# Attention scores with keys on partitions, an unshifted exponential and a general path behind a branch

## Chip, cores and metric

One NeuronCore of one Trainium2 chip. The metric is the device time of one execution in microseconds (us); where several were timed, the median is quoted with the number of executions.

## The reference, cut to what matters

Eight images of 512 channels and 32 x 32 = 1024 positions, all in fp32. First multi-head attention over positions (8 heads of 64 channels), then a second, linear non-local layer and a batch normalization over everything.

```python
q = _conv1x1(x, Wq, bq).reshape(B, h, d, H * W)          # B=8, h=8, d=64, H*W=1024
k = _conv1x1(x, Wk, bk).reshape(B, h, d, H * W)
v = _conv1x1(x, Wv, bv).reshape(B, h, d, H * W)
attn = jax.nn.softmax(jnp.einsum('bhdn,bhdm->bhnm', q, k) * scale, axis=-1)
out = jnp.einsum('bhnm,bhdm->bhdn', attn, v).reshape(B, C, H, W)
x = x + _conv1x1(out, Wp, bp)
# layer 1
theta_x, phi_x, g_x = ...                                 # 1x1 products of x to 256 channels
f_div_C = jnp.einsum('bcn,bdn->bcd', theta_x, phi_x) / n
y = jnp.einsum('bcd,bdn->bcn', f_div_C, g_x)
z = _conv1x1(y, W_w, W_b) + x
return batch_norm(z) * gamma + beta                       # over images and positions
```

## The kernel before

Scores have queries on partitions. Two heads make a pair: they sit in partitions 0 to 63 and 64 to 127, so their score products use the two row halves of TensorE's array. The maximum of a row is taken on VectorE, the exponential with its sum on ScalarE, the scaling on GpSimd. As the value product needs keys on partitions, every attention row is then transposed on TensorE and copied out of PSUM. PSUM holds two score buffers of two banks, and in single banks two for transposes and two for all other products.

```python
psS = ...(name="psS", bufs=2, PSUM)    # score buffers [128, 1024], 2 banks each
psT = ...(name="psT", bufs=2, PSUM)    # transposes
psM = ...(name="psM", bufs=2, PSUM)    # all other products

def scores(p, i, q, k):                # pair p, block i of 128 queries
    ps = [psS.tile([P, N], F32, tag="s") for j in range(2)]
    for nh in range(NH):
        for j in range(2):
            r = slice(j * D, (j + 1) * D)
            nc.tensor.matmul(ps[j][:, nh*512:(nh+1)*512], q[r, i*P:(i+1)*P], k[r, nh*512:(nh+1)*512], ...)
    for j in range(2):
        nc.vector.tensor_reduce(nm, ps[j], AX.X, ALU.max, negate=True)
        nc.scalar.activation(e, ps[j], AF.Exp, bias=nm, accum_out=sm)
        nc.vector.reciprocal(rs, sm)
        nc.gpsimd.tensor_scalar(e, e, rs, 1.0, ALU.mult, ALU.mult)

def values(p, i, es):
    for j in range(2):
        for half in range(2):
            for m in range(NB // 2):
                nc.tensor.transpose(pt[:, m, :], es[j][:, mb * P:(mb + 1) * P], ident)
            # half 0 is copied out by VectorE, half 1 by ScalarE
    if g == GRP - 1:                   # after every second block
        for m in range(NB):
            for j in range(2):         # the two heads: column halves of the array
                nc.tensor.matmul(ps[j*D:(j+1)*D, :GRP*P], v[:, m, h*D:(h+1)*D], pts[j][:, m, :], ...)
# ... cut: projections, layer 1, batch normalization; 5 of 8 images are spilled to DRAM and reloaded
```

Of the kernel before, what the change touches and what calls it, by code (L numbers as in the profile page):

```python
# [8 lines left out]
F32 = mybir.dt.float32  # L9
AF = mybir.ActivationFunctionType  # L10
ALU = mybir.AluOpType
AX = mybir.AxisListType

P = 128
HEADS = 8
EPS = 1e-5


@with_exitstack
def attention_nonlocal_kernel(ctx: ExitStack, tc: tile.TileContext, a: dict, out: bass.AP):  # L20
# [3 lines left out]
    CC = C // P  # channel chunks  # L24
    NB = N // P  # position blocks
    NH = N // 512  # position halves, one PSUM bank each
# [4 lines left out]
    KEEP = 3  # batches whose values stay in SBUF  # L31
    GRP = 2  # position blocks that one attention-value product takes
# [3 lines left out]
    big = ctx.enter_context(tc.tile_pool(name="big", bufs=2))  # L36
    w1 = ctx.enter_context(tc.tile_pool(name="w1", bufs=1))
    w2 = ctx.enter_context(tc.tile_pool(name="w2", bufs=2))
    w3 = ctx.enter_context(tc.tile_pool(name="w3", bufs=3))
    small = ctx.enter_context(tc.tile_pool(name="small", bufs=4))  # L40
    psS = ctx.enter_context(tc.tile_pool(name="psS", bufs=2, space=bass.MemoryType.PSUM))
    psT = ctx.enter_context(tc.tile_pool(name="psT", bufs=2, space=bass.MemoryType.PSUM))
    psM = ctx.enter_context(tc.tile_pool(name="psM", bufs=2, space=bass.MemoryType.PSUM))
    dram = ctx.enter_context(tc.tile_pool(name="dram", bufs=1, space=bass.MemoryType.DRAM))

    x_v = a["x"].rearrange("b (cc p) h w -> b p cc (h w)", p=P)
    out_v = out.rearrange("b (cc p) h w -> b p cc (h w)", p=P)

# [6 lines left out]
    def load_w(name):  # L55
        k, m = a[name].shape
        t = const.tile([P, k // P, m], F32, tag=name, name=name)
        nc.scalar.dma_start(t, a[name].rearrange("(c p) f -> p c f", p=P))
        return t

    def load_col(name):
        t = const.tile(list(a[name].shape), F32, tag=name, name=name)
        nc.sync.dma_start(t, a[name])
        return t

# [1 line left out]
    wv = load_w("WvT")  # L67
    x_next = load_x(0)
    wq, wk = load_w("WqT"), load_w("WkT")
    bv_b = const.tile([P, C], F32, tag="bv_b", name="bv_b")  # L70
    nc.sync.dma_start(bv_b, a["bv"].partition_broadcast(P))
    bq, bk, bp, gb, wb = (load_col(n) for n in ("bq", "bk", "bp", "gb", "Wb"))
    gamma, beta = load_col("gamma"), load_col("beta")
    wp = load_w("WpT")
    tpb = const.tile([P, 2 * CI], F32, tag="tpb", name="tpb")
    nc.sync.dma_start(tpb[:, :CI], a["theta_b"].partition_broadcast(P))
    nc.sync.dma_start(tpb[:, CI:], a["phi_b"].partition_broadcast(P))
# [3 lines left out]
    wg, ww = load_w("WgT"), load_w("WwT")  # L81

    ident = const.tile([P, P], F32, tag="ident", name="ident")
    make_identity(nc, ident)
    eps = const.tile([P, 1], F32, tag="eps", name="eps")
    nc.vector.memset(eps, EPS)
    stats = const.tile([P, CC, B * NH, 6], F32, tag="stats", name="stats")
    spill = [dram.tile([P, CC, N], F32, tag=f"spill{b}", name=f"spill{b}") for b in range(B - KEEP)]

    def mm(m, n, pairs, name):  # L90
        """The sum of products of (lhsT, rhs) over pairs, in one PSUM bank."""
        ps = psM.tile([P, 512], F32, tag="mm", name=name)
        for i, (l, r) in enumerate(pairs):
            nc.tensor.matmul(ps[:m, :n], l, r, start=(i == 0), stop=(i == len(pairs) - 1))  # L94
        return ps[:m, :n]

# [1 line left out]
    def layer0(b, xt):  # L98
        v = big.tile([P, NB, C], F32, tag="big", name=f"v_{b}")  # [position, channel]
        for i in range(NB):  # L100
            ps = mm(P, C, [(xt[:, c, i * P:(i + 1) * P], wv[:, c, :]) for c in range(CC)], f"pv_{b}_{i}")
            nc.vector.tensor_tensor(v[:, i, :], ps, bv_b, ALU.add)

        o = big.tile([P, CC, N], F32, tag="big", name=f"o_{b}")

        def make_qk(p):
            q = w2.tile([P, N], F32, tag="q", name=f"q_{b}_{p}")
            k = w2.tile([P, N], F32, tag="k", name=f"k_{b}_{p}")
            for nh in range(NH):
                s = slice(nh * 512, (nh + 1) * 512)  # L110
                co = slice(p * P, (p + 1) * P)
                ps = mm(P, 512, [(wq[:, c, co], xt[:, c, s]) for c in range(CC)], f"pq_{b}_{p}_{nh}")
                nc.vector.tensor_scalar(q[:, s], ps, bq[:, p:p + 1], float(D) ** -0.5, ALU.add, ALU.mult)  # L113
                ps = mm(P, 512, [(wk[:, c, co], xt[:, c, s]) for c in range(CC)], f"pk_{b}_{p}_{nh}")
                nc.scalar.activation(k[:, s], ps, AF.Identity, bias=bk[:, p:p + 1])  # L115
            return q, k

        def scores(p, i, q, k):
            """The normalized attention rows of position block i, for the two heads of pair p."""
            ps = [psS.tile([P, N], F32, tag="s", name=f"ps_{b}_{p}_{i}_{j}") for j in range(2)]  # L120
            for nh in range(NH):
                for j in range(2):
                    r = slice(j * D, (j + 1) * D)
                    nc.tensor.matmul(  # L124
                        ps[j][:, nh * 512:(nh + 1) * 512],
                        q[r, i * P:(i + 1) * P],
                        k[r, nh * 512:(nh + 1) * 512],
                        start=True, stop=True,
                    )
            res = []  # L130
            for j in range(2):
                nm = small.tile([P, 1], F32, tag="nm", name=f"nm_{b}_{p}_{i}_{j}")
                nc.vector.tensor_reduce(nm, ps[j], AX.X, ALU.max, negate=True)  # L133
                e = w3.tile([P, N], F32, tag="e", name=f"e_{b}_{p}_{i}_{j}")
                sm = small.tile([P, 1], F32, tag="sm", name=f"sm_{b}_{p}_{i}_{j}")
                nc.scalar.activation(e, ps[j], AF.Exp, bias=nm, accum_out=sm)  # L136
                rs = small.tile([P, 1], F32, tag="rs", name=f"rs_{b}_{p}_{i}_{j}")
                nc.vector.reciprocal(rs, sm)  # L138
                nc.gpsimd.tensor_scalar(e, e, rs, 1.0, ALU.mult, ALU.mult)  # L139
                res.append(e)  # L140
            return res

        pts = {}

        def values(p, i, es):
            """Transposes the attention rows; after each GRP blocks, multiplies them with v."""
            g = i % GRP
            if g == 0:
                for j in range(2):
                    pts[j] = w3.tile([P, NB, GRP * P], F32, tag="pt", name=f"pt_{b}_{p}_{i}_{j}")  # L150
            for j in range(2):
                for half in range(2):
                    pt = psT.tile([P, NB // 2, P], F32, tag="t", name=f"pst_{b}_{p}_{i}_{j}_{half}")
                    for m in range(NB // 2):
                        mb = half * (NB // 2) + m
                        nc.tensor.transpose(pt[:, m, :], es[j][:, mb * P:(mb + 1) * P], ident)  # L156
                    dst = pts[j][:, half * (NB // 2):(half + 1) * (NB // 2), g * P:(g + 1) * P]
                    if half == 0:
                        nc.vector.tensor_copy(dst, pt)  # L159
                    else:  # L160
                        nc.scalar.copy(dst, pt)  # L161
            if g == GRP - 1:
                ps = psM.tile([P, 512], F32, tag="mm", name=f"pav_{b}_{p}_{i}")
                for m in range(NB):
                    for j in range(2):
                        h = 2 * p + j
                        nc.tensor.matmul(  # L167
                            ps[j * D:(j + 1) * D, :GRP * P],
                            v[:, m, h * D:(h + 1) * D],
                            pts[j][:, m, :],  # L170
                            start=(m == 0), stop=(m == NB - 1),
                        )
                i0 = i - (GRP - 1)
                nc.vector.tensor_copy(o[:, p, i0 * P:(i + 1) * P], ps[:, :GRP * P])  # L174

        qk = make_qk(0)
        qk_next = None
        pending = None
        for p in range(NPAIR):
            for i in range(NB):  # L180
                es = scores(p, i, *qk)
                if pending is not None:
                    values(*pending)
                pending = (p, i, es)
                if i == NB // 2 and p + 1 < NPAIR:
                    qk_next = make_qk(p + 1)
# [137 lines left out]
```

## Time and profile before

| | before |
|---|---|
| time, 4 executions | 3519.7 to 3556.3 us, median 3554.9 |
| profiled execution | span 3518.2 us, mean granted clock 0.987 |
| TensorE busy | 3226.5 us, 92% |
| after the last matmul | 65 us, DMA share 0.93 to 1.02 at 374 to 411 GB/s |

Three groups of its attention matter for the change (columns: line, engine, operation, operands, count; busy us, mean ns of one; idle time before and what ended it). In timelines further down the first two columns are the start and the duration in us, and brackets give the idle time before and what ended it; PE is TensorE, PEld its weight loads, DVE VectorE, ACT ScalarE, POOL GpSimd:

```profile
L156 PE MATMUL pst<-ident,e 128*128 128x128 f32 x4096 | 560.1, 280 | 17.5 <-ACT pt L161 10.5
L133 DVE TENSOR_REDUCE nm<-ps 128x1 f32<-128x1024 f32 x512 | 602.8, 1219 | 294.0 <-PE ps L124 294.0
L124 PE MATMUL ps<-k,q 64*128 64x512 f32 x2048 | 793.9, 637 | 199.6 <-ACT e L136 199.6
```

4096 transposes, a VectorE pass over all scores, and 200 us in which TensorE stood before a score product until an exponential had freed its buffer.

### The profile page before, as it was taken

The page shows a single profiled execution, that of the slowest core. Times are in us where ns is not written, and L with a number is a line of the kernel's source. Part 1 is how long each engine was busy: PE and PEld are TensorE (multiplying, and loading weights), DVE is VectorE, ACT ScalarE, POOL GpSimd, SP SyncE. Part 2 cuts the span into 40 slices and gives each one's busy share as a digit, 9 for nine tenths or more (in the row PEclk, how much of TensorE's full clock was granted, in tenths as well). Part 3 has the DMA queues.
Part 4 walks back from the last instruction along what each step waited for, and adds up shares of the span by engine and source line. Part 5 has one row for each costly group of instructions (what it writes and reads, how often), then busy time and mean ns, then how long its engine had stood idle before and what let it go on. Part 6 is the DMA issues. An engine that isn't in the chain of part 4 may idle for free.

```text
span 3518.2 us, 33619 instructions
## 1 busy us (share of the span) xinstructions
PE 3226.5 (92%) x13632; PEld 1653.5 (47%) x13632; DVE 1329.1 (38%) x2087; ACT 984.7 (28%) x1699; POOL 574.5 (16%) x518
## 2 busy tenths in 40 slices
PE   8998999999999999999999999999999999999992
PEld 3445444444444544444444444444444445444451
DVE  2344234442344423443234432444324442244424
ACT  2334013330233202332033320333103331133304
POOL 1222012220122201221022210222102220022200
PEclk9999999999999999999999999999999999999996
DMA  4000000000000010000100001000000000000016
GB/s 150 1 1 1 13 35 1 1 1 34 15 1 1 1 48 0 1 1 1 48 0 1 1 1 48 1 1 1 1 0 1 1 1 0 0 1 1 1 48 262
DMA packets 20538, 63.51 MB, mean 18 GB/s; under 512 B 2848, under 2 KB 4640, under 8 KB 20384
## 3 DMA queue, kind: packets, MB, share of 16 engines
q1 hardware_dynamic: 11808, 38.29, 2.9%
q10 hardware_dynamic: 8576, 23.07, 1.7%
q8 instruction: 108, 1.77, 0.2%
q14 instruction: 46, 0.38, 0.0%
HBM read 34.09 MB, written 27.26 MB: 17 GB/s over the span
## 4 chain that ended last, share of the span: by engine, by line
PE 78%; DVE 10%; ACT 9%; issue 1%; DMA 1%; ACTq 0%; SPq 0%
PE ps L124 16%; PE pav L167 15%; DVE nm L133 9%; ACT e L136 9%; PE pst L156 8%; PE pq L94 6%; PE pv L94 6%; PE pp L94 6%; PE pk L94 6%; PE ptp L94 6%; PE pg L94 3%; PE pz L94 3%; PE pf L94 2%; PE pwf L94 1%; DMA z<-spill 1%
## 5 line engine op out<-in xcount | busy, mean ns | idle before, releaser
L139 POOL TENSOR_SCALAR e<-e,rs 128x1024 f32<-128x1024 f32 x512 | 573.8, 1121 | 2779.4 <-DVE rs L138 2779.3
L124 PE MATMUL ps<-k,q 64*128 64x512 f32 x2048 | 793.9, 637 | 199.6 <-ACT e L136 199.6
L136 ACT ACTIVATE e<-ps,nm 128x1024 f32<-128x1024 f32 x512 | 573.7, 1121 | 857.9 <-DVE nm L133 857.9
L133 DVE TENSOR_REDUCE nm<-ps 128x1 f32<-128x1024 f32 x512 | 602.8, 1219 | 294.0 <-PE ps L124 294.0
L156 PEld LDWEIGHTS pst<-ident,e 128*128 128x128 f32 x4096 | 439.6, 141 | 394.6 <-issue 291.8
L156 PE MATMUL pst<-ident,e 128*128 128x128 f32 x4096 | 560.1, 280 | 17.5 <-ACT pt L161 10.5
L167 PE MATMUL pav<-pt,v 128*64 128x256 f32 x4096 | 522.7, 382 | 0.0
L159 DVE COPY pt<-pst 128x512 f32<-128x512 f32 x512 | 351.1, 686 | 329.9 <-PE pst L156 329.9
L124 PEld LDWEIGHTS ps<-k,q 64*128 64x128 f32 x2048 | 252.5, 188 | 473.1 <-ACT e L136 263.4
L167 PEld LDWEIGHTS pav<-pt,v 128*64 128x64 f32 x4096 | 319.8, 137 | 166.2 <-DVE pt L159 28.8
L161 ACT COPY pt<-pst 128x512 f32<-128x512 f32 x512 | 297.7, 581 | 178.8 <-PE pst L156 178.8
L115 ACT ACTIVATE k<-pk,bk 128x512 f32<-128x512 f32 x64 | 44.0, 687 | 800.4 <-PE pk L94 800.4
L174 DVE COPY o<-pav 128x256 f32<-128x256 f32 x128 | 54.3, 424 | 472.8 <-PE pav L167 472.8
L94 PE MATMUL pq<-x,WqT 128*128 128x512 f32 x512 | 232.7, 597 | 0.0
L94 PE MATMUL pv<-WvT,x 128*128 128x512 f32 x512 | 222.7, 596 | 9.1 <-DMA WvT<-in_WvT_dram 9.1
L94 PE MATMUL pk<-x,WkT 128*128 128x512 f32 x512 | 230.2, 592 | 0.0
L94 PE MATMUL pp<-o,WpT 128*128 128x512 f32 x512 | 221.9, 594 | 0.0
L94 PE MATMUL ptp<-wtp,x 128*128 128x512 f32 x512 | 221.0, 592 | 0.0
L94 PEld LDWEIGHTS pv<-WvT,x 128*128 128x128 f32 x512 | 97.8, 191 | 132.0 <-issue 122.8
L113 DVE TENSOR_SCALAR q<-pq,bq 128x512 f32<-128x512 f32 x64 | 48.0, 750 | 294.7 <-PE pq L94 294.7
L94 PEld LDWEIGHTS pk<-x,WkT 128*128 128x128 f32 x512 | 97.3, 190 | 122.5 <-issue 122.5
L94 PEld LDWEIGHTS ptp<-wtp,x 128*128 128x128 f32 x512 | 97.3, 190 | 122.5 <-issue 122.5
(37 smaller groups left out, 1170.9 us busy)
## 6 DMA issues: line engine op xcount, KB each, us to landing
x<-in_x_dram SPq DMA_DIRECT2D x32, 512.0 KB, 5.8
spill<-x SPq DMA_DIRECT2D x20, 512.0 KB, 2.6
z<-spill SPq DMA_DIRECT2D x20, 512.0 KB, 6.8
out_dram<-z ACTq DMA_DIRECT2D x20, 512.0 KB, 5.4
out_dram<-x ACTq DMA_DIRECT2D x12, 512.0 KB, 5.2
WvT<-in_WvT_dram ACTq DMA_DIRECT2D x1, 1024.0 KB, 8.4
WqT<-in_WqT_dram ACTq DMA_DIRECT2D x1, 1024.0 KB, 13.9
WkT<-in_WkT_dram ACTq DMA_DIRECT2D x1, 1024.0 KB, 16.0
```

The costliest lines, as they stand in the source:

```text
L94: nc.tensor.matmul(ps[:m, :n], l, r, start=(i == 0), stop=(i == len(pairs) - 1))
L113: nc.vector.tensor_scalar(q[:, s], ps, bq[:, p:p + 1], float(D) ** -0.5, ALU.add, ALU.mult)
L115: nc.scalar.activation(k[:, s], ps, AF.Identity, bias=bk[:, p:p + 1])
L124: nc.tensor.matmul(ps[j][:, nh * 512:(nh + 1) * 512], q[r, i * P:(i + 1) * P], k[r, nh * 512:(nh + 1) * 512], start=True, stop=True,)
L133: nc.vector.tensor_reduce(nm, ps[j], AX.X, ALU.max, negate=True)
L136: nc.scalar.activation(e, ps[j], AF.Exp, bias=nm, accum_out=sm)
L139: nc.gpsimd.tensor_scalar(e, e, rs, 1.0, ALU.mult, ALU.mult)
L156: nc.tensor.transpose(pt[:, m, :], es[j][:, mb * P:(mb + 1) * P], ident)
L159: nc.vector.tensor_copy(dst, pt)
L161: nc.scalar.copy(dst, pt)
L167: nc.tensor.matmul(ps[j * D:(j + 1) * D, :GRP * P], v[:, m, h * D:(h + 1) * D], pts[j][:, m, :], start=(m == 0), stop=(m == NB - 1),)
L174: nc.vector.tensor_copy(o[:, p, i0 * P:(i + 1) * P], ps[:, :GRP * P])
```

## The change

Scores are made transposed: keys on partitions, queries along the free dimension. The exponential then has the layout that the value product wants as its moving operand, and transposes and copies fall away. A row's maximum would now lie across partitions, so the shift is left out. To make that safe, each pair's scores are bounded by the sum over channels of max|q| max|k|; if any bound exceeds 60, the queries are zeroed and a complete second program (`shifted`) runs at the end behind a branch. Sums come from additions on VectorE and a product with ones, and the division is applied to the output. PSUM now holds three score buffers of two banks, used for all large products too, and two single banks. TensorE's order is pinned; other products stand where a result is awaited. The core of the diff:

```diff
-    psS = ctx.enter_context(tc.tile_pool(name="psS", bufs=2, ...PSUM))
-    psT = ...bufs=2;  psM = ...bufs=2
+    psS = ctx.enter_context(tc.tile_pool(name="psS", bufs=3, space=PSUM))
+    psO = ctx.enter_context(tc.tile_pool(name="psO", bufs=2, space=PSUM))
+    RUN = 4      # steps (pair, query half, key block) in a run
+    LEAD = 128
+    def pe(ins): tc.keep_in_program_order(ins)
+    # queries_keys(): max|k|, max|q| by tensor_reduce, their product is `peak`
+    def bound_scores(b, p, q, k, peak):
+        pe(nc.tensor.matmul(ps[:, 0, :1], heads, peak, start=True, stop=True))
+        nc.vector.tensor_scalar(gate, ps[:, 0, :1], BOUND, 1.0, ALU.is_le, ALU.mult)
+        nc.gpsimd.tensor_scalar(q, q, gate, 1.0, ALU.mult, ALU.mult)
+    def scores(run):
+        for p, h, m in run:
+            for j in range(2):
+                pe(nc.tensor.matmul(ps[:, j, :], k[r, m*P:(m+1)*P], q[r, h*512:(h+1)*512], ...))
+            nc.scalar.activation(e, ps, AF.Exp)
+            nc.vector.tensor_tensor(acc, acc, e, ALU.add)
+    def columns(ps, lhsT, rhs, start, stop, lead):
+        for j in range(2):
+            if lead and j == 0:        # first product of a run in two pieces, 128 and 384 columns
+                pe(nc.tensor.matmul(to[:, :LEAD], l, r[:, :LEAD], ...))
+                pe(nc.tensor.matmul(to[:, LEAD:], l, r[:, LEAD:], ...))
+            else:
+                pe(nc.tensor.matmul(to, l, r, ...))
+    def normalize(p, h, lead):
+        columns(ps, lambda j: ones, lambda j: acc[:, j, :], True, True, lead)
+        nc.vector.reciprocal(ri, ps)
+        nc.vector.tensor_tensor(o[:, p, s], o[:, p, s], ri, ALU.mult)
+    for i, run in enumerate(runs):
+        scores(run)
+        if i % 4 == 3 ...: bound_scores(b, p + 1, *qk[p + 1])
+        if i: weighted(runs[i - 1], due)   # value products; starts with normalize() when one is due
+        if i % 4 == 2 ...: qk[p + 1] = queries_keys(b, xt, p + 1)
+    # next image's values and queries fill gaps of layer 1; 6 images are spilled and reloaded early
+    sound = nc.values_load(count, min_val=0, max_val=P)
+    with tc.If(sound < P): shifted(tc, a, out)
```

## The prediction

VectorE's 12.9 us per half pair and the gate's 7.9 us count the additions, whose time came from no trace, and so do the 26 to 30 us per pair and the 46% of the span. Read from the trace of the kernel before: 512 `pq` instructions for 256 fp32 products, hence two for each; the reciprocal's 177 - 153 = 24 ns for three more elements. The 0.4 us for a bound, the 0.1 us of scattered waits per run and the 2 to 4 us for landing and the branch are estimates, and so are the 3 us of slow clock; for these, that trace has the first weight loads 0.85 us apart instead of 0.43 until 11.9 us, and a granted clock of 0.50 from 57 to 60.

> **What bounds the kernel now.** I read the page first, for who is busy.
>
> ```profile
> span 3518.2 us, 33619 instructions
> PE 3226.5 (92%) x13632; PEld 1653.5 (47%) x13632; DVE 1329.1 (38%) x2087; ACT 984.7 (28%) x1699; POOL 574.5 (16%) x518
> PE 78%; DVE 10%; ACT 9%; issue 1%; DMA 1%; ACTq 0%; SPq 0%
> ```
>
> TensorE is at 92%, and the chain that ended last is its work for 78%. The other 19% are VectorE and ScalarE steps (the maximum, the exponential) that TensorE waits for. So two things count: how much TensorE has to do, and whether something still interrupts it. The groups of instructions give the first, with a warning: matmul spans overlap, so I do not take durations from means but from distances between starts. For these I read TensorE's timeline inside the attention of image 1.
>
> ```profile
> 601.46 3.60 PE L94 MATMUL pk<-x,WkT 128*128 128x512 f32 x8
> 604.89 3.60 PE L94 MATMUL pq<-x,WqT 128*128 128x512 f32 x8
> ...
> 613.76 1.09 PE L156 MATMUL pst<-ident,e 128*128 128x128 f32 x8
> 615.60 1.12 PE L124 MATMUL ps<-k,q 64*128 64x512 f32 x2 [0.75 <-ACT e L136]
> 616.65 1.09 PE L156 MATMUL pst<-ident,e 128*128 128x128 f32 x8
> 617.68 1.98 PE L124 MATMUL ps<-k,q 64*128 64x512 f32 x6
> 619.59 1.09 PE L156 MATMUL pst<-ident,e 128*128 128x128 f32 x8
> 621.43 1.12 PE L124 MATMUL ps<-k,q 64*128 64x512 f32 x2 [0.75 <-ACT e L136]
> 622.48 1.09 PE L156 MATMUL pst<-ident,e 128*128 128x128 f32 x8
> 623.50 4.08 PE L167 MATMUL pav<-pt,v 128*64 128x256 f32 x32
> 627.52 1.98 PE L124 MATMUL ps<-k,q 64*128 64x512 f32 x6
> 629.43 1.09 PE L156 MATMUL pst<-ident,e 128*128 128x128 f32 x8
> ```
>
> Four readings. (1) Eight full-array instructions take 604.89 - 601.46 = 3.43 us, 0.4288 each; an fp32 product is two of them, 0.857 us for 512 columns. (2) The value product is 32 instructions of 256 columns. At the full-array rate they would take 32 x 0.214 = 6.86 us; they take 627.52 - 623.50 = 4.02, so the two heads, in two column halves of the array, do run side by side. (3) Of a block's eight score instructions only four overlap: six take 1.91 us and two, alone, 1.05, while four perfect pairs would be 4 x 0.4288 = 1.72. The scheduler had to break the second pair because its PSUM buffer was still read by the exponential (the 0.75 us). (4) The pattern repeats every two blocks: 629.43 - 613.76 = 15.67 us. There are 128 such repeats (8 images x 4 pairs x 4), so attention proper is 128 x 15.67 = 2006 us. Full-array products are 3136 instructions of 512 columns (x0.4288 = 1345 us) and 256 of 256 columns (55 us): 1400 us. Together 3406; the rest is start (9 us to the first matmul), edges of each image and the end.
>
> The end I read from windows of busy time (columns: stretch, length, PE, PEld, DVE, ACT, POOL busy, granted clock, DMA share, GB/s):
>
> ```profile
> 3460.00:3480.00 20.00, 0.00 (x0) 0.00 (x0) 13.52 (x19) 12.49 (x13) 0.00 (x0) 0.50 1.00 374
> 3480.00:3500.00 20.00, 0.00 (x0) 0.00 (x0) 6.50 (x8) 9.12 (x9) 0.00 (x0) 0.50 1.02 411
> 3500.00:3518.00 18.00, 0.00 (x0) 0.00 (x0) 0.00 (x0) 10.41 (x10) 0.00 (x0) 0.50 0.93 379
> ```
>
> After the last matmul (3453) 65 us follow, and the DMA engines are full at about 390 GB/s: 16.8 MB go out while 12 chunks of spilled z (6.3 MB) still come in.
>
> [...] heads in column halves start late, 4.02 us against 3.43 for perfect pairs. [...] Eight transposes of 128 columns need 8 x 0.107 = 0.86 us at the rate of reading 1, and from 622.48 to 623.50 1.02 passed: I estimate 0.1 to 0.16 us per change. [...] The trace has it for one element (153 ns) and for four (177 ns): 8 ns an element[...]. So a reciprocal of 512 columns should cost about 4.2 us. [...]
>
> **The change, part by part.** *The branch to the general path is not taken.* I computed the bound from the reference's inputs: 18.6 to 20.5 over all images and head pairs, against a limit of 60. The second program costs only its reading of a count and one branch per engine.
>
> *Removed from TensorE:* all transposes, 4096 x 0.107 = 440 us plus their mode changes, and the exponential's 0.75 us, twice in 15.67 (192 us). Also removed: VectorE's maximum (602.8 us) and its copies (351), ScalarE's copies (298) and accumulator reads (103), GpSimd's scaling (574).
>
> *Scores.* Per image there are 64 steps (pair, half, key block), each one pair of 512-column products in the two row halves. Runs of four steps: 8 x 0.4288 = 3.43, plus about 0.19 for the change of mode in and out, 3.62 us. 128 runs: 463 us. Each step has its own two-bank buffer of three, so nothing breaks the pairs: the fourth step starts 2.57 us into a run and needs the first exponential to be over (product done at about 1.05, plus 1.12: 2.2).
>
> *Value product.* Runs of four steps in column halves: 8 x 0.4288, plus the late start of the second head (0.42 us in the trace's first such group; the 128-column lead may shorten it) and a change: about 3.95 us. 128 runs: 506 us.
>
> *Sums.* Sixty-four pairs of products with ones: 64 x 0.86 = 55 us. New, on TensorE.
>
> *Unchanged:* 1400 us of full-array products, now emitted in an order that puts other products wherever a result is awaited (next image's values and queries).
>
> *Bounds.* 32 tiny products with what they wait for, 0.4 us each: 13 us.
>
> *Other engines.* A score and a value run together last 7.6 us. ScalarE has four exponentials then, 4.5 us. VectorE has, per half pair (15.2 + 0.86 us, plus 13.7/2 of queries and keys in three of four pairs), [...] one reciprocal of 4.3 and a multiplication of 0.6, 12.9 us, and for the next pair q's eviction and two maxima, 3.7 us per pair. So 26 to 30 us of 32 to 46. VectorE is the nearest rival, but its work has runs of slack. The gate is the tightest: from the end of q's product, eviction 1.3, maximum 1.2, [...] gate, GpSimd 1.12, 7.9 us; the scores that need q come at about 8.5.
>
> *End.* Six images reload during the last image's second layer (12.6 MB, some 32 us at 390 GB/s, of about 90 us); 16.8 MB then leave in 43 us; with 5 us ahead and 2 to 4 for landing and the branch, 50 instead of 65.
>
> *Sum.* 1400 + 463 + 506 + 55 + 13 = 2437. Start 17 (9 as now, 3 of slow clock, 5 for the first bound with nothing to hide it). Last image without filler products: 8 (its last reciprocal and multiplication 5, f and wf 3). Scattered waits, 0.1 us per run, 13. End 50. Span 2525 us. The measured time now is 3556 - 3518 = 38 us over the span; kept, that gives 2563. I put 2560.
>
> **Rivals.** (a) *VectorE becomes the bound.* If an addition took 1.5 us or the reciprocal blocked the gate, each of 24 pair changes would lose 2 to 4 us, and each half pair some more: 2640 to 2750. For it: in-order VectorE holds an addition behind each reciprocal. Against: its sum is 46% of the span. (b) *Heads do not pair over long runs,* [...] value runs of up to 6 us, 128 x 2 = 260 us more, 2820. Against: reading 2, where the steady rhythm is paired. (c) *ScalarE paces the runs:* 1.12 us per step against TensorE's 0.86. If the buffer's slack of about 0.3 us is eaten by semaphores, each run loses some tenths: 128 x 0.3 = 40 us, 2600. (d) *All waits vanish, the lead removes the second head's delay:* 2500. A slower result would need the general path to run, which the bound excludes.
>
> **Range and chances.** The sum of TensorE's own work, 2424, is counted from starts in the trace and hardly wrong by 2%; what is uncertain is waiting, which only adds. So 2490 to 2680, chance 8 in 10, with (a) and (b) above it. Faster by over 2%: 0.98.
>
> **What would show it.** Transposes gone, TensorE over 93% busy; score groups of eight instructions every 3.5 to 3.7 us, value groups about 4.0; reciprocal near 4.3 us; [...] waits of TensorE below 40 us outside start and end; the end after the last matmul near 50. Wrong if value groups exceed 4.5 us, if VectorE tops 80% inside attention, or if TensorE waits for the exponential in each run.

## The result

| | before | after |
|---|---|---|
| time, median of 4 | 3554.93 us (3519.71 to 3556.32) | 2469.09 us (2468.91 to 2469.50) |
| span of the profiled execution | 3518.2 us | 2467.0 us |

The ratio is 0.6968 (95% interval 0.6928 to 0.7008): the mean time of one kernel's fast runs over that of the other's of the same rounds, so not quite the ratio of the medians. Faster, as predicted, but 91 us below the predicted 2560 and under the lower end of the range, 2490. The page of the kernel after: span, busy time by engine, and the chain that ended last.

```profile
span 2467.0 us, 19195 instructions
PE 2402.4 (97%) x8066; PEld 1032.8 (42%) x8066; DVE 1139.7 (46%) x973; ACT 622.5 (25%) x675; POOL 36.0 (1%) x36
PE 97%; ACT 1%; DMA 0%; DVE 0%; issue 0%; POOL 0%; ACTq 0%
```

The chain that ended last is now TensorE alone, and TensorE waits for almost nothing. Its timeline inside the attention of image 1 shows score runs (`ps`) and value runs (`po`) one behind the other:

```profile
664.52 0.32 PE L186 MATMUL po<-e,v 128*64 128x128 f32 x1
664.53 0.64 PE L189 MATMUL po<-e,v 128*64 128x512 f32 x1
...
665.44 2.75 PE L189 MATMUL po<-e,v 128*64 128x512 f32 x12
668.11 3.70 PE L170 MATMUL ps<-q,k 64*128 64x512 f32 x16
671.75 0.32 PE L186 MATMUL po<-e,v 128*64 128x128 f32 x1
```

A value run takes 668.11 - 664.52 = 3.59 us, a score run 671.75 - 668.11 = 3.64. The two heads of a value run start 0.01 us apart (664.52 and 664.53).

To see where the time went I added up, in both traces, the distance from each matmul's start to the next one's, by what the matmul writes (so a wait counts to the group before it):

| us | before | after | difference |
|---|---|---|---|
| until the first matmul | 9 | 5 | -4 |
| scores (`ps`) | 781 | 466 | -315 |
| transposes (`pst`) | 739 | 0 | -739 |
| value products (`pav`, `po`) | 514 | 455.5 | -58 |
| sums and bounds | 0 | 69 | +69 |
| full-array products | 1409 | 1419 | +10 |
| after the last matmul begins | 66 | 51.5 | -14 |
| span | 3518 | 2467 | -1051 |

The transposes with the waits behind them are 70% of the gain and the scores another 30%; the value product's small gain nearly pays for sums and bounds. The scores' 315 us are mostly whole pairs. Some 40 of them lie at the starts of the eight images' attention, where the first 16 score instructions, with their wait, took 7.6 to 9.4 us. The products that now fill such places were not taken out in any run, so what they are worth by themselves is not measured.

### The profile page after: what moved, and what is told of

It reads as the page before. It is cut to its first block, busy times and chain, and to the rows that moved or that the text cites. A ratio compares the mean times of both kernels' runs of the same rounds, so it can differ in the third digit from the quotient of the medians.

```text
span 2467.0 us, 19195 instructions
## 1 busy us (share of the span) xinstructions
PE 2402.4 (97%) x8066; PEld 1032.8 (42%) x8066; DVE 1139.7 (46%) x973; ACT 622.5 (25%) x675; POOL 36.0 (1%) x36
## 4 chain that ended last, share of the span: by engine, by line
PE 97%; ACT 1%; DMA 0%; DVE 0%; issue 0%; POOL 0%; ACTq 0%
PE ps L170 19%; PE po L189 17%; PE pk L116 9%; PE pp L116 9%; PE pq L116 9%; PE ptp L116 9%; PE pv L116 9%; PE pz L116 4%; PE pg L116 4%; PE pf L261 2%; PE psum L189 1%; PE pwf L116 1%; PE po L187 1%; ACT z L356 1%; PE po L186 1%; PE psum L187 1%
## 5 line engine op out<-in xcount | busy, mean ns | idle before, releaser
L173 ACT ACTIVATE e<-ps 128x1024 f32<-128x1024 f32 x512 | 482.5, 1033 | 578.3 <-PE ps L170 578.2
L179 DVE TENSOR_TENSOR acc<-acc,e 128x1024 f32<-128x1024 f32 x384 | 466.7, 1215 | 104.9 <-ACT e L173 76.0
L170 PE MATMUL ps<-q,k 64*128 64x512 f32 x2048 | 474.4, 604 | 1.5 <-POOL q L155 1.5
L189 PE MATMUL po<-e,v 128*64 128x512 f32 x1904 | 464.3, 594 | 0.0
L170 PEld LDWEIGHTS ps<-q,k 64*128 64x128 f32 x2048 | 187.7, 187 | 283.9 <-issue 205.3
L189 PEld LDWEIGHTS po<-e,v 128*64 128x64 f32 x1904 | 153.3, 137 | 211.9 <-issue 200.7
L197 DVE RECIPROCAL ri<-psum 128x512 f32<-128x512 f32 x64 | 214.4, 3349 | 24.1 <-PE psum L189 24.1
L116 PEld LDWEIGHTS pq<-x,WqT 128*128 128x128 f32 x512 | 97.3, 190 | 122.5 <-issue 122.5
L116 PEld LDWEIGHTS pp<-o,WpT 128*128 128x128 f32 x512 | 96.7, 190 | 119.4 <-issue 119.4
L238 DVE SCALAR_TENSOR_TENSOR x<-pp,bp,x 128x1024 f32<-128x1024 f32 x32 | 41.1, 1284 | 166.5 <-PE pp L116 166.5
```

The source lines that it names most:

```text
L116: pe(nc.tensor.matmul(ps[:, h, :], l, r, start=(i == 0), stop=(i == len(pairs) - 1)))
L170: pe(nc.tensor.matmul(ps[:, j, :], k[r, m * P:(m + 1) * P], q[r, h * 512:(h + 1) * 512], start=True, stop=True))
L173: nc.scalar.activation(e, ps, AF.Exp)
L179: nc.vector.tensor_tensor(accs[p, h], accs[p, h], e, ALU.add)
L189: pe(nc.tensor.matmul(to, l, r, start=start, stop=stop, skip_group_check=True))
L197: nc.vector.reciprocal(ri, ps)
```

## The experiments

All twelve gave correct results. Each was timed in alternation with the kernel before on the same chip.

**The kernel before, again.** No edit. The prediction had added 38 us, the distance between its profiled span and the median time.

> The kernel before, unchanged, to see what the 38 us are that the prediction carried over between its profiled span (3518 us) and its measured time (3556 us). If they are a fixed cost outside the span, every run shows a span near 3518 and a time near 3555. Rival: they are a longer execution, so runs of 3555 us have spans of about 3553 and runs of 3520 us spans of about 3518, perhaps at another granted clock; then nothing was to be carried over.

Measured: 3555.8 us (4 executions, 3525.2 to 3564.7). Each execution's span is 1.7 or 1.8 us below its time: 3563.0 and 3564.74 at a granted clock of 0.972, 3523.4 and 3525.20 at 0.986. So there is no fixed cost outside the span; the kernel before has longer and shorter executions. Where they part, windows around the start of image 1's attention show (columns: stretch, length, PE, PEld, DVE, ACT, POOL busy, granted clock, DMA share, GB/s). First the profiled 3518 us execution, then the one of 3563:

```profile
486.00:494.00 8.00, 6.91 (x17) 3.91 (x18) 4.09 (x7) 3.56 (x7) 2.52 (x3) 0.57 0.00 0
494.00:530.00 36.00, 33.75 (x167) 17.81 (x166) 13.92 (x24) 12.90 (x23) 8.68 (x8) 1.00 0.00 1
```

```profile
492.00:514.00 22.00, 22.00 (x62) 11.34 (x64) 7.95 (x14) 7.94 (x14) 6.70 (x6) 0.53 0.00 1
514.00:540.00 26.00, 24.50 (x121) 12.83 (x118) 9.17 (x15) 7.43 (x13) 4.47 (x4) 1.00 0.00 1
```

The clock falls to about half when an image's attention begins, for some 7 us in one execution and some 20 in the other. From 40 us to the last matmul, half clock lasts 27 us in all in the first and 140 us in the second, nearly all of it at these starts. In the first these stretches last 3.41 us (four) or 6.83 us (two). What goes before it is TensorE's first long wait, for the first maximum and exponential, as the timeline of the 3518 us execution has it:

```profile
482.49 1.99 PE L124 MATMUL ps<-k,q 64*128 64x512 f32 x8
487.09 4.91 PE L124 MATMUL ps<-k,q 64*128 64x512 f32 x8 [2.61 <-ACT e L136]
```

The second eight score instructions take 4.91 us instead of 1.99. In the kernel after other products stand at that place, and its clock is at 1.00 from 61 us to 2400:

```profile
53.00:61.00 8.00, 5.70 (x16) 2.79 (x18) 1.07 (x4) 2.05 (x3) 1.12 (x1) 0.57 0.00 0
61.00:500.00 439.00, 439.00 (x1568) 185.72 (x1566) 226.65 (x189) 130.97 (x143) 7.82 (x7) 1.00 0.03 10
500.00:2400.00 1900.00, 1899.31 (x6356) 819.72 (x6352) 867.11 (x720) 451.12 (x493) 26.82 (x24) 1.00 0.05 18
```

Three runs described below, which were built for other questions, bear on whether the wait brings the lower clock. Without the maximum, the same wait is 1.26 us instead of 2.61; no stretch at half clock is left before the last matmul (mean granted clock 0.991 instead of 0.987), and four executions lie within 1.2 us. Without the bound, the wait of 2.9 us for it at the start is gone, and so is the stretch at 53 us (mean granted clock 0.990 instead of 0.989). With every reciprocal done twice, TensorE gets a new wait of 3.75 us in the last image's projection, and there a new stretch at lower clock follows. First the start of image 1's attention without the maximum, then the place of the new wait:

```profile
470.00:490.00 20.00, 18.51 (x93) 8.87 (x91) 3.65 (x10) 9.31 (x17) 6.66 (x6) 1.00 0.00 1
```

```profile
2332.00:2336.00 4.00, 4.00 (x7) 1.56 (x6) 1.28 (x1) 0.00 (x0) 0.00 (x0) 0.57 0.93 288
```

So the lower clock comes and goes with the longer waits in these runs, though none of them changes a wait and nothing else, and not every such wait brings it: image 2 of the profiled 3518 us execution has the same wait of 2.61 us and no lower clock behind it. Why it lasts 7 us in some executions and 20 in others stays open.

**No lead.**

```diff
-                if lead and j == 0:
+                if False:
```

> The changed kernel with the 128-column lead taken away: the first product of every value run is one of 512 columns in both heads. Theory of the prediction (the second head of a column pair starts 0.42 us late [...] and the lead is what removed that): value runs grow from 3.59 to about 4.0 us, 128 of them, so some 50 us more, 2520 us. Rival (the late start in the kernel before was a wait for VectorE's copy of the second head's transposes, and column halves need no lead): value runs stay within 0.05 us of 3.59 and the time within 7 us of 2469.

Measured: 2468.3 us. TensorE's timeline of this kernel:

```profile
666.75 3.65 PE L189 MATMUL po<-e,v 128*64 128x512 f32 x16
670.33 3.70 PE L170 MATMUL ps<-q,k 64*128 64x512 f32 x16
```

Without a lead a value run takes 670.33 - 666.75 = 3.58 us. The lead is worth nothing, and no head of a column pair starts late here: sixteen instructions with their weight loads take 3.58 us where perfect pairs would take 3.43, and the 0.15 us are about a change of tiling (0.18, see the runs of two steps). What the prediction had taken for a cost of column halves was a wait; it stands in the timeline of the kernel before, one line from the one it had quoted:

```profile
623.17 0.69 DVE L159 COPY pt<-pst 128x512 f32<-128x512 f32 x1 [1.30 <-PE pst L156]
623.50 0.19 PEld L167 LDWEIGHTS pav<-pt,v 128*64 128x64 f32 x2 [0.17 <-issue]
...
623.92 3.21 PEld L167 LDWEIGHTS pav<-pt,v 128*64 128x64 f32 x30 [0.23 <-DVE pt L159]
```

The first head's two weight loads start at 623.50; the others wait for the copy of the second head's transposes, which ends at 623.86.

**Two score buffers.**

```diff
-    psS = ctx.enter_context(tc.tile_pool(name="psS", bufs=3, space=PSUM))
+    psS = ctx.enter_context(tc.tile_pool(name="psS", bufs=2, space=PSUM))
```

> The changed kernel with two instead of three score buffers in PSUM (2 banks each). Theory (the third buffer lets TensorE run ahead of the exponential): the third step of a run waits for the first exponential and the fourth for the second, runs of scores grow from 3.63 to about 4.0 us, and the bound's product waits too; 50 us more, about 2520 us. Rival (ScalarE's 0.94 us per exponential against TensorE's 0.86 is close enough that two buffers do): under 15 us more.

Measured: 2577.7 us, 109 more; twice what I expected. In its timeline the third step waits:

```profile
697.07 1.99 PE L170 MATMUL ps<-q,k 64*128 64x512 f32 x8
699.38 2.04 PE L170 MATMUL ps<-q,k 64*128 64x512 f32 x8 [0.33 <-ACT e L173]
701.36 0.32 PE L186 MATMUL po<-e,v 128*64 128x128 f32 x1
```

A score run takes 4.29 us here (701.36 - 697.07), 4.23 in the median against 3.63. Scores grow by 99 us in all and bounds by 10. So in the changed kernel the third score buffer is worth a tenth of the gain; its two banks are those that the transposes had. (This run uses two banks fewer than either kernel, so it is not the old layout.)

**The kernel before without its maximum.**

```diff
-                nc.vector.tensor_reduce(nm, ps[j], AX.X, ALU.max, negate=True)
-                nc.scalar.activation(e, ps[j], AF.Exp, bias=nm, accum_out=sm)
+                nc.scalar.activation(e, ps[j], AF.Exp, accum_out=sm)
```

> The kernel before with only the maximum taken out: exp without shift, scores still with queries on partitions, transposes still there (the result stays right for these inputs). It tells what leaving out the shift alone is worth. If the wait for the exponential was all: its 200 us of idle time go, span near 3320 us. If the broken score pairs come together again as well (a block's scores in 1.8 instead of 2.96 us, 256 blocks): down to about 3030 us. Rival: the exponential still follows the scores and GpSimd's scaling still stands before the transposes, so the order only shifts its waits and under 100 us are won; then nearly the whole gain comes from the transposed layout.

Measured: 3417.6 us, ratio 0.9659 (0.9592 to 0.9727), 105 us below the 3523 of the kernel before's shorter executions. The wait for the exponential went, the rest did not come:

```profile
L124 PE MATMUL ps<-k,q 64*128 64x512 f32 x2048 | 817.0, 633 | 38.6 <-ACT e L134 38.6
```

Idle time before scores fell from 199.6 to 38.6 us, yet scores hold 785 us of TensorE, as before (781): the scheduler put lone score products between transposes, with more changes of tiling. The transposes still take 611 us. Leaving out the shift is worth a tenth of the gain by itself, part of it because the stretches at half clock went too; its main use is that it allows the transposed layout.

**Runs of two steps.**

```diff
-    RUN = 4
+    RUN = 2
-            if i % 4 == 3 and p + 1 < NPAIR:     # bound
+            if i % 8 == 7 and p + 1 < NPAIR:
-            if i % 4 == 2 and p + 1 < NPAIR:     # queries and keys
+            if i % 8 == 5 and p + 1 < NPAIR:
```

> The changed kernel with runs of two steps instead of four, so twice as many changes between row halves (scores) and column halves (values); queries and keys of the next pair are made one run earlier, in time for their bound. Theory of the prediction (0.1 us per change of tiling, counted in as 0.19 per score run and 0.09 to 0.16 per value run): runs of 1.72 us grow to about 1.9 and 1.88, 256 more changes cost 40 to 50 us, about 2515 us. Rival (the changes are hidden, and the 0.2 us over 3.43 in each run is something else, such as the wait for the exponential): under 15 us more, since shorter runs also relieve the exponential.

Measured: 2556.2 us, 87 more. In the median a score run takes 1.92 us (half of a long one is 1.815) and a value run 1.87 (1.795). There are 256 runs of each kind instead of 128, so 256 more changes of tiling cost 256 x (0.105 + 0.075) = 46 us, as expected: 0.18 us each, which is also what a run of four has over its 3.43 us (0.16 for values, 0.20 for scores). What such a change consists of, these runs do not show. The other 41 are something I had not expected; the waits of this kernel have it (us in total, times, longest):

```profile
PEld ps L170 <- POOL q L155: 62.5, 25, 2.6
```

With short runs less work stands between a bound and the scores behind it, and they wait for the gated queries (21.0 us in all in the kernel after). The gating itself is longer too: 2.08 us instead of 1.12 in the 24 instances that stand beside an addition on VectorE, so 24 x 0.96 = 23 us of the 41. In a run of four it stands beside a reciprocal and keeps its 1.12 us. So the order of a run of four hides the gate.

**Every reciprocal twice.**

```diff
             nc.vector.reciprocal(ri, ps)
+            nc.vector.reciprocal(ri, ps)
```

> The changed kernel with every reciprocal done twice over (same result): 64 times 3.35 us, 214 us more of VectorE. Theory (VectorE has slack, rival (a) of the prediction is wrong): span grows by under 15 us, mostly the one exposed reciprocal at the end of the last image (3.4 us) and some waits of sums for additions. Rival (a) (in-order VectorE holds the additions, the gates and the sums back): 24 pair changes and 64 halves lose 1 to 3 us each, 60 to 150 us more.

Measured: 2476.5 us, 7 more for 214 us of VectorE work; the longest new wait, 3.75 us, stands in the last image's projection, which awaits the last division and has no filler. VectorE, busy for 55% of this run's span, is not the bound.

**No bound, and no bound and no branch.**

```diff
-            nc.vector.tensor_reduce(peak[i], t, AX.X, ALU.max, apply_absolute_value=True)
-        nc.vector.tensor_tensor(peak[0], peak[0], peak[1], ALU.mult)
     def bound_scores(b, p, q, k, peak):
-        (the bound's product, gate and multiplication)
+        return
+    nc.vector.memset(gates, 1.0)
```

and in the second also

```diff
-    sound = nc.values_load(count, min_val=0, max_val=P)
-    with tc.If(sound < P):
-        shifted(tc, a, out)
```

Both are right for these inputs only.

> The changed kernel without the proof: no maxima of queries and keys, no bound product, no gate on the queries; the gates are set to one, so the count and the branch stay. Not a valid kernel in general, right for these inputs. The bound products take 10.5 us of TensorE's time in the trace, and the first pair's wait some 5 us that nothing hides: 12 to 16 us less, about 2455 us. Rival (bounds also delay the queries of the next pair and the sums behind them): over 30 us less.

> As the one before it, and the general path and its branch are taken out as well: its difference to that one is what reading a count and jumping over a second program cost at the end. The trace shows the last DMA landing about 51 us after the last matmul, of which 43 are the writing of the result: I expect 0 to 3 us between the two. Rival [...]: 5 us or more.

Measured: 2454.3 and 2452.2 us. The proof costs 15 us, the branch with the second program 2: 0.7% for generality.

**Free order.**

```diff
     def pe(ins):
-        tc.keep_in_program_order(ins)
+        return ins
```

> The changed kernel with TensorE's program order left to the scheduler, as in the kernel before; everything else as it is. Theory (the pinned order matters, because runs of four keep score pairs whole and tiling changes few): the scheduler breaks runs and pairs as it did in the kernel before, 100 us or more. Rival (transposed layout and three buffers suffice, and the scheduler finds as good an order): within 30 us of 2469.

Measured: 2467.1 us, and the order that the scheduler chose differs only at the first values and at the count. The expected 100 us did not come: the pinning does nothing here, and the program's own order is kept without it.

**Sums in two bf16 parts.**

```diff
-            columns(ps, lambda j: ones, lambda j: acc[:, j, :], True, True, lead)
+            nc.gpsimd.tensor_copy(hi, acc)                         # bf16
+            nc.gpsimd.tensor_tensor(lo, acc, hi, ALU.subtract)     # bf16
+            columns(ps, lambda j: ones16, lambda j: hi[:, j, :], True, False, False)
+            columns(ps, lambda j: ones16, lambda j: lo[:, j, :], False, True, False)
     # and normalize() is issued behind the value run instead of ahead of it
```

> A try at a version faster than both: the sums of exponentials are split by GpSimd into two bf16 parts (high and rest), whose products with ones take one array pass each instead of the two double ones of fp32, and the division is issued behind a value run instead of ahead of it, to give GpSimd time. Sums should fall from 58.9 us of TensorE to about 33: 20 to 28 us less, about 2445 us, if GpSimd's two passes stay beside the rest. Rival ([...] the later division holds the sums' buffer): no gain or a loss. The rest keeps 16 bits of each sum, so the result should stay correct.

Measured: 2466.7 us, no gain. The products did get short: one instruction of 512 bf16 columns for each, the next pair 0.21 us later (711.62 and 711.83), where an fp32 product takes two of 0.4288. But TensorE now waits for the gated queries. Two groups of this kernel, two lines of its timeline, and the gating in the kernel after:

```profile
L173 PE MATMUL ps<-q,k 64*128 64x512 f32 x2048 | 474.1, 603 | 25.0 <-POOL q L158 25.0
L158 POOL TENSOR_SCALAR q<-q,gates 128x1024 f32<-128x1024 f32 x32 | 60.0, 1876 | 894.2 <-DVE gates L157 894.2
```

```profile
695.00 1.23 DVE L182 TENSOR_TENSOR acc<-acc,e 128x1024 f32<-128x1024 f32 x1
695.14 2.08 POOL L158 TENSOR_SCALAR q<-q,gates 128x1024 f32<-128x1024 f32 x1 [22.83 <-DVE gates L157]
```

```profile
696.21 1.12 POOL L155 TENSOR_SCALAR q<-q,gates 128x1024 f32<-128x1024 f32 x1 [136.09 <-DVE gates L154]
```

The gating did not stand behind the split: GpSimd had been idle for 22.83 us and started when the gate was there. But it took 2.08 us instead of 1.12, and TensorE waits 25 us for it in all. As the division is now issued behind the value run, an addition on VectorE stands beside the gating where a reciprocal stood before. It takes 2.08 to 2.16 us in the 24 instances beside an addition and 1.12 in the eight with nothing beside them. This is what the runs of two steps showed as well; why the gating is longer there was not tested. A wait had taken the place of the work removed.

**The same, with the gate on ScalarE,** which is busy for a quarter of the time.

```diff
-        nc.gpsimd.tensor_scalar(q, q, gate, 1.0, ALU.mult, ALU.mult)
+        nc.scalar.activation(q, q, AF.Copy, scale=gate)
```

> The bf16 sums again, with the gate multiplied into the queries by ScalarE instead of GpSimd. In the run before, the sums' own products fell to 24.8 us each half of the split and overlapped, but the scores waited 25 us for the gated queries, because GpSimd stood in the split of a sum. Theory (that wait is all that ate the gain): the 25 us go and about 2442 us remain. Rival [...]: the gain stays under 10 us.

Measured: 2442.3 us (6 executions, 2441.2 to 2443.9), ratio to the kernel before 0.6902. Its groups:

```profile
L173 PE MATMUL ps<-q,k 64*128 64x512 f32 x2048 | 474.8, 604 | 1.7 <-ACT q L158 1.7
```

The recorded reason, that GpSimd stood in the split, was not right (see above), but the remedy was: on ScalarE the gating takes 1.15 us beside the same addition. The first additions of a half stay long (1434 ns, 1441 in the run before, 1222 in the kernel after), and the gain comes all the same. The wait is gone, sums hold 34 us of TensorE instead of 59, and the kernel is 26 us faster than the changed one (2468.7 us when run again in rounds of its own, below): the fastest valid version found. It keeps the bound and the general path; its sums keep some 16 bits of each fp32 value.

**The changed kernel again.**

> The changed kernel, unchanged, once more: it runs each of its executions with the clock lowered only at the start and the end, so its times should again lie within 2 us of 2469 while those of the kernel before spread over 3520 to 3560. If instead it too shows executions some 30 us longer, the comparison with the last run (2442 us) needs care.

Measured: 2468.7 us (2468.2 to 2469.6), while the kernel before ranged from 3518.6 to 3540.3 beside it.

## Why the prediction was wrong

The direction was right, and so was the mechanism of the gain: transposes and waits go, and TensorE stays the bound. Two steps failed, the 38 us carried over and the cost of a value run, and the number was 91 us too high. Its sum was 2563 (put as 2560), 94 over the result. By its own terms:

| term | predicted | measured | error |
|---|---|---|---|
| time over span | 38 | 2 | -36 |
| value runs | 506 | 455.5 | -50.5 |
| full-array products, start, last image, scattered waits | 1438 | 1424 | -14 |
| scores, sums, bounds | 531 | 535.5 | +4.5 |
| end | 50 | 51.5 | +1.5 |

**"The measured time now is 3556 - 3518 = 38 us over the span; kept."** Wrong in kind. The span came from a short execution and the median from long ones; execution by execution the two agree within 2 us (e0). The longer ones lose their time to a lower clock at the start of each image's attention, and the kernel after, with no such gap, has one kind of execution only.

**"The late start of the second head (0.42 us in the trace's first such group)."** The value run of 3.95 us should have been 3.59. The delay was real, its cause misread: a data wait on VectorE's copy, which the change removes with the transposes. That weight loads held the second head back was not shown by any trace, and reading 1 spoke against it: full-array products follow each other every 0.4288 us with a weight load of 0.19 us in each step. The lead, which looked like a remedy, does nothing (e1). This is over half of the error.

**"Start 17", 8 us for the last image, 13 of scattered waits.** Over-counted by 14 us. The first matmul starts at 5 us instead of 9. The other allowances came to 29 us (3 of slow clock, 5 for the first bound, 8 and 13), and full-array products, with the waits that count to them, hold 19 us over the 1400. "Waiting only adds" was the wrong guard: the largest errors lay in the counted part.

Right: score runs 3.62 against 3.64; transposes gone; chain of TensorE; end 50 against 51.5; VectorE with slack (e5); cost of a tiling change (e4); branch not taken and 2 us (e7). The addition took 1.215 us and the reciprocal 3.35 instead of 4.3: with 153 ns for one column and 3349 for 512 it is 6.25 ns a column, not the 8 read from one and four; neither mattered. Of the rivals, (a), (b) and (c) did not happen, though an addition does stand behind a reciprocal, as (a) said: in the kernel after one starts at 714.19 us, when a reciprocal of 3.35 us from 710.92 ends, and its exponential was over at 709.84; (d), "all waits vanish", came nearest, with 2500, and was held up by the same 38 us; part of its reason, the lead, was wrong, so its nearness is in part luck. The buffer slack in (c) is real: with one buffer less it costs 109 us (e2).

## What to carry to other kernels

If a product's result has to be transposed before its next use, swap its operands so that it comes out transposed; what then stands in the way (here the row maximum) may be replaced by a bound, which cost 0.7%. Before calling a late start a limit of the hardware, look at what the weight load just before it waits for. And compare a span only with the time of the same execution; look at the granted clock before carrying a difference over.
